# Four 2D scans at the end of a convolution stack: one-number reads ahead of the additions, half-tile row loads, a row-ordered result and moved early buffers

## Chip, cores and metric

One NeuronCore of one Trainium2 chip runs the whole program in one launch. The metric is device time in microseconds; the kernel before takes 9100.21 us (median of 3 runs, 9092.29 to 9107.42).

## What is computed

x has the shape [4, 48, 256, 256], float32. Layers 0 and 1 (an attention layer and a gated layer, both with convolutions) end as x2. Layers 2 and 3 are the scans; each normalizes its input by groups and adds the scan's result to it:

```python
def step(w, b):
    def f(carry, inp):
        nxt = inp + _conv1d(carry, w, b)      # 48 -> 48 channels, 5 taps along the line
        return (nxt, nxt)
    return f
# down over the rows, back up over them with the same weights,
# then right over the columns, then left: 4 x 256 dependent steps for each layer
x = x + _L2_conv_ref(_gn(x), ...)
x = x + _L3_conv_ref(_gn(x), ...)
```

Every step needs the line that the step before made, so a scan is a chain: multiplication on TensorE, addition on VectorE, the next multiplication.

## The kernel before

The four images form two pairs, and each pair is one generator, `chain(pair)` (L1015). A line is kept as 96 partitions (two neighbouring positions by 48 channels) by 2 images by 128 elements. `step` (L1037) makes one scan step: for each image i, three `nc.tensor.matmul` into a PSUM bank (L1045; the trace has two records for each, so 6 for a half step and 12 for a step), one `tensor_add` of PSUM and the input line into the next of four carry buffers (L1049 or L1053, NC = 4), then a callback `after` that files the line: ScalarE writes it with its bias into the row or column tile (L1127 down, L1168 up, L1248 right), and in the left scan GpSimd adds it to the residual (L1293, or L1297 into the `done` tile when it goes straight to the output: `direct`, L1271, layer 3 of the second pair). All of a step's engines wait for each other by semaphores that the framework places.

Tiles are slots of 16 KB a partition, five in a ring for each pair (`take`, L1012). In the down scan a tile of 32 rows is two slots (even and odd rows); `load_rows` (L1069) brings the next tile's two slots with 8 DMAs at row 0 of a tile, and `norm` (L1101, ScalarE, L1104) scales each quarter of them at rows 16, 20, 24 and 28. D, U and Rt are DRAM copies of the scans' results, stored tile by tile. Where the up scan ends and the right scan begins (the turn, L1150 to L1211), the first column block `column` is put together from U and from the tile at hand; later blocks are loaded from U (L1235). GpSimd copies each column to a contiguous `pre` tile three steps ahead (`fetch`, L1221, four buffers). In the left scan of layer 2, batch statistics of finished blocks run on VectorE between the steps (L1325).

The first pair's final result is stored in column blocks as `xs[2]` (L1309); `to_rows` (L1369) loads it again in pieces of 512 bytes, GpSimd (three) and ScalarE (one) copies it into row order (L1393, L1395), and it is stored (L1397). The second pair writes the output itself (`write`, L1312), 128 bytes at a time, and 64 bytes for the last two blocks.

The order: all DMAs of the scans are issued on SyncE's queue, in one static order. The framework lists instructions greedily: a list scheduler with a cost model places what is ready, by priority, which is program order unless `high_priority` moves it. Program order of the chains is at L1400 to L1415: the first loads of chain 0 with priority 1600 places earlier, the first loads of chain 1, 992 steps of chain 0 (`LEAD`), then both in turn, then the rest of chain 1 with a piece of `to_rows` at the steps in `times`. So chain 0 (layer 2) runs nearly alone from 3543 to 4990 us, both chains run together until about 7530 us, and chain 1 (layer 3) runs alone to the end.

Of the kernel before, what the change touches and what calls it, by code (L numbers as in the profile page):

```python
# [964 lines left out]
def scans(ctx, tc, xs, out, wts, biases, dram, k, coefs, lead, spare):  # L965
# [23 lines left out]
    work = pool("c_work", 2)  # L989
# [12 lines left out]
    HP = W // 2 + 2  # L1002

# [11 lines left out]
    def chain(pair):  # L1015
# [6 lines left out]
        at = [0]  # L1022

# [45 lines left out]
        def load_rows(layer, n, ts, k0, k1):  # L1069

            for r in range(2):
                v = rows_view(ts[r])
                for q in range(2):
                    for b in range(2):
                        nc.sync.dma_start(
                            v[q * C : (q + 1) * C, b, k0:k1].rearrange("c k h w -> c k (h w)"),
                            xs[layer][pair][
                                r * C : (r + 1) * C, b, 2 * k0 + q : 2 * k1 - 1 + q : 2, n * NH : (n + 1) * NH, :
                            ].rearrange("c k h w -> c k (h w)"),
                        )  # L1080

        def layer_of(layer, first):
# [18 lines left out]
            def norm(ts, r, b):  # L1101
                v = by_batch(ts[r])[:, b]
                g = biased[b]
                nc.scalar.activation(v, v, AF.Identity, bias=g[:, 1:2], scale=g[:, 0:1])  # L1104
# [7 lines left out]
            for r in range(2):  # L1112
                for b in range(2):
                    norm(now, r, b)
            for n in range(NT):
                ahead_ = None
                for r in range(RT):
                    if r == 0 and n + 1 < NT:
                        ahead_ = [slot("dn"), slot("dn")]
                        load_rows(layer, n + 1, ahead_, 0, NK)  # L1120
                    if ahead_ and r >= RT // 2 and r % 4 == 0:
                        i = (r - RT // 2) // 4
                        norm(ahead_, i // 2, i % 2)
# [7 lines left out]
                    else:  # L1131
                        step(layer, 0, inp, keep)
                    yield
# [8 lines left out]
            column = None  # L1142
            for n in reversed(range(NT)):
                ahead_ = None
                for r in reversed(range(RT)):
# [4 lines left out]
                    if n == 0 and r == RT // 4:  # L1150

                        column = slot("col")
                        v = cols_view(column)
                        for par in range(2):
                            for b in range(2):
                                h0 = NH + 1 - par
                                here = slice(par * C, (par + 1) * C)
                                nc.sync.dma_start(
# [381 lines left out]
```

## Time and profile before

| what | value |
|---|---|
| median of 3 runs | 9100.21 us (9092.29 to 9107.42) |
| profiled execution, its own time | 9095.42 us |
| its span, clock | 9093.6 us, 0.982 |
| busy share PE / DVE / ACT / POOL | 96% / 41% / 38% / 23% |
| records of the scans' matmuls (L1045) | 48960 |
| addition, 96x128 (L1049, L1053) | 286 to 288 ns |
| ScalarE's filing of a line (L1127, L1168, L1248) | 398 to 402 ns |
| GpSimd's addition (L1293), copy to `pre` (L1225), copy to rows (L1393) | 519, 644, 1130 ns |
| `norm` of a quarter tile (L1104) | 2081 ns, 128 of them |
| one-number copy or addition on VectorE (L1097, L1098) | 0.14 to 0.16 us |

In a line of a table by stretches stand: the stretch and its length, the busy time of PE with its records in brackets, the same for weight loads (PEld), the granted clock, the busy share of the DMA engines and GB/s. In a line of the timeline stand start, duration, engine (SPq: SyncE's queue; DVEq: VectorE's sequencer), line, operation and, in square brackets, the engine's idle time before it and what ended it. A merged line covers several instructions ("x2").

### The profile page before, as it was taken

The page shows a single profiled execution, that of the slowest core. Times are in us where ns is not written, and L with a number is a line of the kernel's source. Part 1 is how long each engine was busy: PE and PEld are TensorE (multiplying, and loading weights), DVE is VectorE, ACT ScalarE, POOL GpSimd, SP SyncE. Part 2 cuts the span into 40 slices and gives each one's busy share as a digit, 9 for nine tenths or more (in the row PEclk, how much of TensorE's full clock was granted, in tenths as well). Part 3 has the DMA queues.
Part 4 walks back from the last instruction along what each step waited for, and adds up shares of the span by engine and source line. Part 5 has one row for each costly group of instructions (what it writes and reads, how often), then busy time and mean ns, then how long its engine had stood idle before and what let it go on. Part 6 is the DMA issues. An engine that isn't in the chain of part 4 may idle for free.

```text
span 9093.6 us, 162344 instructions
## 1 busy us (share of the span) xinstructions
PE 8711.1 (96%) x62920; PEld 7268.3 (80%) x62920; DVE 3759.8 (41%) x10790; ACT 3489.6 (38%) x7033; POOL 2067.0 (23%) x3855
## 2 busy tenths in 40 slices
PE   6999999999999987999999999999999999999997
PEld 4777777433333345999999999999999999999997
DVE  3332010234555555444455444444445554343443
ACT  0011000123343355755511776665662004665510
POOL 0000000001111120002465000002446773002475
PEclk9999999999999988999999999999999999999998
DMA  7663323467878878655587773656556787888689
GB/s 150 132 135 87 74 59 73 97 136 168 181 171 187 177 165 165 149 133 128 145 211 178 157 147 95 160 129 160 154 152 177 218 227 169 172 183 201 175 173 168
DMA packets 1201990, 1390.61 MB, mean 153 GB/s; under 512 B 285712, under 2 KB 1128208, under 8 KB 1138240
## 3 DMA queue, kind: packets, MB, share of 16 engines
q1 hardware_dynamic: 1201120, 1379.90, 67.3%
q8 instruction: 493, 8.08, 0.4%
q14 instruction: 281, 2.30, 0.1%
q0 software_dynamic: 96, 0.33, 0.0%
HBM read 812.02 MB, written 509.61 MB: 145 GB/s over the span
## 4 chain that ended last, share of the span: by engine, by line
PE 88%; DMA 4%; DVE 3%; ACT 1%; issue 1%; SPq 1%; POOL 1%; DVEq 0%; POOLq 0%; ACTq 0%
PE ps L1045 57%; PE py L581 7%; PE acc L294 6%; PE acc L295 5%; PE acc L296 4%; PE py L590 3%; PE pt L276 1%; DMA stage<-x 1%; DMA tok<-x 1%; PE ph L698 1%; PE pout L868 1%; DMA x<-y 1%; PE ptok L751 1%; ACT x1n L541 1%; DMA sx<-in_x 1%
## 5 line engine op out<-in xcount | busy, mean ns | idle before, releaser
L1045 PE MATMUL ps<-carry,w 96*96 96x128 f32 x48960 | 5496.1, 275 | 75.6 <-DVE carry L1049 29.7
L1045 PEld LDWEIGHTS ps<-carry,w 96*96 96x96 f32 x48960 | 5445.9, 163 | 129.1 <-DVE carry L1053 39.6
L1225 POOL COPY pre<-col 96x256 f32<-96x256 f32 x1020 | 655.1, 644 | 2800.1 <-DMA col<-last 2011.7
L1248 ACT ACTIVATE lines<-carry,b 96x128 f32<-96x128 f32 (+1 forms) x2044 | 817.0, 402 | 618.8 <-DVE carry L1053 615.2
L1127 ACT ACTIVATE dn<-carry,b 96x128 f32<-96x128 f32 (+1 forms) x2044 | 770.1, 398 | 712.0 <-DVE carry L1049 709.2
L1049 DVE TENSOR_TENSOR carry<-ps,dn 96x128 f32<-96x128 f32 x2280 | 654.7, 288 | 900.5 <-PE ps L1045 806.8
L1053 DVE TENSOR_TENSOR carry<-ps,pre 96x128 f32<-96x128 f32 x2040 | 586.1, 287 | 798.7 <-PE ps L1045 544.8
L1168 ACT ACTIVATE up<-carry,b 96x128 f32<-96x128 f32 x1792 | 718.1, 402 | 480.1 <-DVE carry L1049 479.0
L1293 POOL TENSOR_TENSOR stage<-stage,carry 96x128 f32<-96x128 f32 (+1 forms) x1533 | 790.7, 519 | 314.2 <-DVE carry L1053 184.3
L1053 DVE TENSOR_TENSOR carry<-ps,lines 96x128 f32<-96x128 f32 x2040 | 576.2, 286 | 671.8 <-PE ps L1045 636.8
L1049 DVE TENSOR_TENSOR carry<-ps,up 96x128 f32<-96x128 f32 x1792 | 515.8, 288 | 678.9 <-PE ps L1045 667.9
L581 PE MATMUL py<-x1n,wy 128*96 128x512 f32 x1536 | 705.2, 609 | 29.1 <-ACT x1n L541 27.9
L295 PE MATMUL acc<-xs,xt 128*96 128x288 f32 x2048 | 666.4, 407 | 0.0
L294 PE MATMUL acc<-xt 128*96 128x288 f32 x2048 | 665.9, 408 | 0.0
L581 PEld LDWEIGHTS py<-x1n,wy 128*96 128x96 f32 x1536 | 245.2, 166 | 453.4 <-issue 436.1
L261 ACT ACTIVATE xn<-raw,coef 96x2048 f32<-96x2048 f32 x64 | 133.6, 2093 | 985.8 <-PE pt L276 818.2
L296 PE MATMUL acc<-xt,xs 128*96 128x192 f32 x2048 | 501.8, 327 | 0.0
L279 DVE COPY xt<-pt 128x384 f32<-128x384 f32 x256 | 136.5, 554 | 848.1 <-PE pt L276 649.4
L296 PEld LDWEIGHTS acc<-xt,xs 128*96 128x96 f32 x2048 | 332.0, 164 | 154.2 <-issue 1.2
L295 PEld LDWEIGHTS acc<-xs,xt 128*96 128x96 f32 x2048 | 331.8, 164 | 151.0 <-issue 2.0
L604 DVE TENSOR_TENSOR y<-py,t 96x512 f32<-96x512 f32 x256 | 171.4, 678 | 596.8 <-PE py L590 596.8
L590 PE MATMUL py<-x2n,wy 64*96 64x512 f32 x1536 | 363.0, 601 | 0.0
(179 smaller groups left out, 4823.8 us busy)
## 6 DMA issues: line engine op xcount, KB each, us to landing
stage<-x SPq DMA_DIRECT2D x64, 1536.0 KB
dn<-x SPq DMA_DIRECT2D x240, 384.0 KB
col<-U SPq DMA_DIRECT2D x60, 1536.0 KB
R<-lines SPq DMA_DIRECT2D x60, 1536.0 KB
lines<-R SPq DMA_DIRECT2D x60, 1536.0 KB
D<-dn SPq DMA_DIRECT2D x56, 1536.0 KB
up<-D SPq DMA_DIRECT2D x56, 1536.0 KB
U<-up SPq DMA_DIRECT2D x224, 384.0 KB
```

The source lines that it names most:

```text
L294: nc.tensor.matmul(acc[0], lhsT=xt[:, h + 2, :], rhs=xt[:, here, :], start=first, stop=last)
L295: nc.tensor.matmul(acc[1], lhsT=xt[:, h + 2, :], rhs=xs[:, here, :], start=first, stop=last)
L296: nc.tensor.matmul(acc[2], lhsT=xs[:, h + 2, :], rhs=xt[:, past, :], start=first, stop=last)
L581: nc.tensor.matmul(ps, lhsT=held["w"][0][:, dx], rhs=x1n[:, 2 * c : 2 * c + 2, dx : dx + W], start=dx == 0, stop=False)
L1045: nc.tensor.matmul(ps, lhsT=w_sb[layer][:, way, j, :], rhs=old[:, i, j : j + W // 2], start=j == 0, stop=j == 2)
L1049: nc.vector.tensor_add(new[:, i].rearrange("p (k w) -> p k w", w=KC), ps.rearrange("p (k w) -> p k w", w=KC), inp[:, i])
L1053: nc.vector.tensor_add(new[:, i], ps, inp[:, i])
L1127: nc.scalar.activation(inp[:, b], blocks(new[:, b]), AF.Identity, bias=bias[:, 0:1])
L1168: nc.scalar.activation(place[:, b], blocks(new[:, b]), AF.Identity, bias=bias[:, 1:2])
L1225: nc.gpsimd.tensor_copy(t, cols_view(block)[:, :, w % 2, :, w // 2])
L1248: nc.scalar.activation(line[:, b], new[:, b], AF.Identity, bias=bias[:, 2:3])
L1293: nc.gpsimd.tensor_add(to[:, b], to[:, b], new[:, b])
```

## The change

1. `look` reads one number of a place that ScalarE (down, up, right) filed three steps earlier into the tile `seen`, once after each step; in the right scan it reads a number of the next `pre` tile as well. In the left scan (not the direct one) VectorE reads a number of the residual at every second step, one such place later. The list is emptied at the start of each row tile and of each scan. In the left scan GpSimd adds both images in one operation.
2. `load_rows` loads one slot; at row 0 of tile n half tiles up to number 2n + 4 are asked for, half a tile more than before. `norm` comes at rows 11, 14, 22, 25.
3. At the turn the first two column blocks are put together from the tile at hand.
4. The first pair has three `pre` buffers instead of four, and fetches two steps ahead. The `work` pool has one buffer instead of two.
5. The first pair's layer 3 is stored as `result` in the order of row blocks, in pieces of 512 bytes, four DMAs a block; `to_rows` loads it in runs of 16 KB a partition. Its first 16 pieces have all four copies on GpSimd; the last 8 start at step 530 instead of 508.
6. The second pair writes the output 128 bytes at a time to the end.
7. Chain 0's first step has priority 1400 places earlier; chain 1's first loads come 64 steps ahead of the end of chain 0's lead.

```diff
...
     first_w = pool("c_first", 1)
     slots_a = pool("c_slot_a", 3)
     wp = pool("c_w", 1)
-    work = pool("c_work", 2)
+    work = pool("c_work", 1)
     slots_b = pool("c_slot_b", 1)
     slots_c = pool("c_slot_c", 1)
     slots_d = pool("c_slot_d", 5)
...
     NC = 4
     HP = W // 2 + 2
+    NY = H // 2 // (SLOT // W)
+    result = dram.tile([P, 2, NY, NK * 2, SLOT // (NK * 2)], F32, tag="result", name="result")
     w_sb, b_sb = [], []
     for layer in range(2):
         at = wp if layer else first_w
...
             nc.gpsimd.memset(c, 0.0)
         last = wp.tile([P, 2, W // 2], F32, tag=f"last{pair}", name=f"last{pair}")
         at = [0]
+        seen = wp.tile([P, 1], F32, tag=f"seen{pair}", name="seen")
+        kept = []
+        def look(place, fetched=None):
+            kept.append(place)
+            if len(kept) > 3:
+                if fetched is None:
+                    nc.vector.tensor_copy(seen, kept.pop(0))
+                else:
+                    nc.vector.tensor_add(seen, kept.pop(0), fetched)
         def slot(name):
             return take(pair, f"{name}{pair}")
...
         def row(ts, r):
             return rows_view(ts[r % 2])[:, :, :, r // 2, :]
...
+        def load_rows(layer, n, r, t, k0, k1):
...
         def layer_of(layer, first):
...
                 nc.vector.tensor_add(t[:, 1:2], g[:, 1:2], bias[:, 0:1])
                 biased.append(t)
...
             for n in range(NT):
                 ahead_ = None
                 for r in range(RT):
-                    if r == 0 and n + 1 < NT:
-                        ahead_ = [slot("dn"), slot("dn")]
-                        load_rows(layer, n + 1, ahead_, 0, NK)
-                    if ahead_ and r >= RT // 2 and r % 4 == 0:
-                        i = (r - RT // 2) // 4
-                        norm(ahead_, i // 2, i % 2)
+                    if r == 0:
+                        kept.clear()
+                        while len(halves) < min(2 * n + 5, 2 * NT):
+                            t = slot("dn")
+                            load_rows(layer, len(halves) // 2, len(halves) % 2, t, 0, NK)
+                            halves.append(t)
+                        if n + 1 < NT:
+                            ahead_ = halves[2 * n + 2 : 2 * n + 4]
+                    if ahead_ and r in (11, 14, 22, 25):
+                        norm(ahead_[r // 22], r % 11 // 3)
                     inp = row(now, r)
                     def keep(new, b):
...
                         keep(inner(), slice(0, 2))
                     else:
                         step(layer, 0, inp, keep)
+                    look(inp[:, 1, 0, 0:1])
                     yield
                 if ahead_:
                     for r in range(2):
...
             nc.scalar.activation(last, inner(), AF.Identity, bias=bias[:, 0:1])
-            column = None
+            columns = None
             for n in reversed(range(NT)):
                 ahead_ = None
+                kept.clear()
                 for r in reversed(range(RT)):
                     if r == RT - 1 and n > 0:
                         ahead_ = [slot("up"), slot("up")]
...
                             nc.sync.dma_start(ahead_[i], D[n - 1][i])
                     if n == 0 and r == RT // 4:
...
+                        columns = [slot("col") for _ in range(2)]
+                        for j in range(2):
...
+                    look(place[:, 1, 0, 0:1])
                     yield
                     if n == 0 and r < 2:
                         par, h0 = 1 - r, r
-                        v = cols_view(column)
+                        for j in range(2):
+                            v = cols_view(columns[j])
+                            for q in range(2):
+                                nc.sync.dma_start(
+                                    v[par * C : (par + 1) * C, :, q, h0 : h0 + NH, :].rearrange("c b h w -> c b (h w)"),
+                                    rows_view(now[r])[q * C : (q + 1) * C, :, j].rearrange("c b h w -> c b (h w)"),
+                                )
+                if n == 0:
...
+                    for j in range(2):
                         for q in range(2):
                             nc.sync.dma_start(
...
+                                cols_view(columns[j])[0:C, :, q, 0, :],
+                                last[q * C : (q + 1) * C, :, j * KC : (j + 1) * KC],
                             )
...
                 for r in range(2):
                     v = rows_view(now[r])
                     par = 1 - r
...
             for _ in range(3):
                 yield
-            x, y = xs[layer][pair], xs[layer + 1][pair]
+            x = xs[layer][pair]
+            y = xs[1][pair]
             stage = None
             fetched = {}
+            tags = [f"st{pair}0", f"st{pair}1"] + [f"pre{pair}{i}" for i in range(1 + pair)]
+            far = len(tags) - 1
             def fetch(block, n, w):
                 g = n * CB + w
-                tag = (f"st{pair}0", f"st{pair}1", f"pre{pair}0", f"pre{pair}1")[g % 4]
-                t = wp.tile([P, 2, W // 2], F32, tag=tag, name="pre")
+                t = wp.tile([P, 2, W // 2], F32, tag=tags[g % len(tags)], name="pre")
                 nc.gpsimd.tensor_copy(t, cols_view(block)[:, :, w % 2, :, w // 2])
                 fetched[g] = t
-            for w in range(1, 3):
+            kept.clear()
+            column = columns[0]
+            for w in range(1, far):
                 fetch(column, 0, w)
             for n in range(NK):
                 ahead_ = None
                 for w in range(CB):
-                    if w == 0 and n + 1 < NK:
+                    if w == 0 and n == 0:
+                        ahead_ = columns[1]
+                    elif w == 0 and n + 1 < NK:
...
                     if w == 0:
                         lines = slot("lines")
-                    if w + 3 < CB:
-                        fetch(column, n, w + 3)
+                    if w + far < CB:
+                        fetch(column, n, w + far)
                     elif ahead_ is not None:
-                        fetch(ahead_, n + 1, w + 3 - CB)
+                        fetch(ahead_, n + 1, w + far - CB)
                     line = lines_view(lines)[:, w]
                     def keep(new, b):
...
                         keep(inner(), slice(0, 2))
                     else:
                         step(layer, 1, fetched.pop(n * CB + w), keep)
+                    if n + 1 < NK or w + 1 < CB:
+                        look(line[:, 1, 0:1], fetched[n * CB + w + 1][:, 1, 0:1])
                     yield
                 if ahead_ is not None:
                     nc.sync.dma_start(Rt[n], lines)
...
+            kept.clear()
             direct = layer == 1 and pair == NP - 1
-            done, width = None, 0
+            done = None
             writes = []
             for n in reversed(range(NK)):
                 ahead_ = None
-                if direct and n < 2:
-                    done, width = take(0, "done").rearrange("p (b n) -> b p n", b=2), CB
-                elif direct and n % 2 == 1:
-                    done, width = [take(0, "done") for _ in range(2)], 2 * CB
+                if direct and n % 2 == 1:
+                    done = [take(0, "done") for _ in range(2)]
                 for w in reversed(range(CB)):
                     if w == CB - 1 and n > 0:
                         ahead_ = slot("lines"), slot("stage")
...
                         nc.sync.dma_start(by_batch(ahead_[1]), block_of(x, n - 1))
                     if layer == 0 and n == 0 and w == CB // 2:
                         following = [slot("dn"), slot("dn")]
-                        load_rows(1, 0, following, 1, NK)
+                        for r in range(2):
+                            load_rows(1, 0, r, following[r], 1, NK)
                     line = lines_view(lines)[:, w]
                     to = cols_view(stage)[:, :, w % 2, :, w // 2]
                     def keep(new, b):
                         if not direct:
-                            nc.gpsimd.tensor_add(to[:, b], to[:, b], new[:, b])
+                            if b.stop == 2:
+                                nc.gpsimd.tensor_add(to, to, new)
                             return
                         for i in range(b.start, b.stop):
-                            place = done[i].rearrange("p (h w) -> p h w", w=width)[:, :, n * CB % width + w]
+                            place = done[i].rearrange("p (h w) -> p h w", w=2 * CB)[:, :, n % 2 * CB + w]
                             nc.gpsimd.tensor_add(place, to[:, i], new[:, i])
                     if n == NK - 1 and w == CB - 1:
                         keep(inner(), slice(0, 2))
                     else:
                         step(layer, 2, line, keep)
+                    if not direct and w % 2:
+                        kept.append(to[:, 1, H // 2 - 1 :])
+                        if len(kept) > 1:
+                            nc.vector.tensor_copy(seen, kept.pop(0))
                     if late:
                         late.pop(0)()
-                    if writes and (w % 4 == 0 if n < 2 else w % 8 == 4):
+                    if writes and w % 8 == 4:
                         writes.pop(0)()
                     yield
-                if not direct:
+                if layer == 0:
                     nc.sync.dma_start(block_of(y, n), by_batch(stage))
-                elif n * CB % width == 0:
-                    def write(b, r, done=done, width=width, w0=n * CB):
+                elif not direct:
+                    v = stage.rearrange("p (b q t n) -> p b q t n", b=2, q=2, t=NY)
+                    for b in range(2):
+                        for q in range(2):
+                            nc.sync.dma_start(result[:, b, :, 2 * n + q], v[:, b, q])
+                elif n % 2 == 0:
+                    def write(b, r, done=done, w0=n * CB):
...
                     writes += [lambda b=b, r=r, f=write: f(b, r) for b in range(2) for r in range(2)]
...
                 yield following
...
-    def to_rows(pair):
-        y = xs[2][pair]
+    def to_rows(pair, engines):
         nh = SLOT // W
         to = out[rows(pair)].rearrange("p (h w) -> p h w", w=W)
-        for n in range(H // 2 // nh):
+        for n in range(NY):
             got = []
             for r in range(2):
                 t = take(pair, "oi")
                 for b in range(2):
                     nc.sync.dma_start(
-                        t[b * C : (b + 1) * C].rearrange("c (k n) -> c k n", k=2 * NK),
-                        y[r * C : (r + 1) * C, b, :, n * nh : (n + 1) * nh, :].rearrange("c k h w -> c k (h w)"),
+                        t[b * C : (b + 1) * C], result[r * C : (r + 1) * C, b, n].rearrange("c k n -> c (k n)")
                     )
                 got.append(t.rearrange("p (k q h w) -> p k q h w", k=NK, q=2, w=KC))
             yield
...
                 for i in range(4):
                     r, q = i // 2, i % 2
                     dst, src = v[:, :, r, :, :, q], got[r][:, :, q, here, :].rearrange("p k h w -> p h k w")
-                    if i < 3:
-                        nc.gpsimd.tensor_copy(dst, src)
+                    if engines[i] is nc.scalar:
+                        nc.scalar.copy(dst, src)
                     else:
-                        nc.scalar.copy(dst, src)
+                        engines[i].tensor_copy(dst, src)
...
     with tc.high_priority(offset=1600):
         next(chains[0])
-    next(chains[1])
-    for _ in range(lead):
+    with tc.high_priority(offset=1400):
+        next(chains[0])
+    for i in range(1, lead):
+        if i == lead - 2 * RT:
+            next(chains[1])
         next(chains[0])
     while next(chains[0], True) is None:
         next(chains[1])
-    pieces = to_rows(0)
-    times = [20 + 26 * i for i in range(16)] + [508 + 28 * i for i in range(8)]
+    engines = [nc.gpsimd] * 4
+    pieces = to_rows(0, engines)
+    times = [20 + 26 * i for i in range(16)] + [530 + 24 * i for i in range(8)]
     for i, _ in enumerate(chains[1]):
+        if i == times[16]:
+            engines[3] = nc.scalar
         if i in times:
             next(pieces, None)
     assert next(pieces, True) is True
...
-        for i in (2, 3, 4)
+        for i in (2, 3)
     ]
     def gated(ctx, tc, banks, p_small):
```

## Prediction

> **What bounds the kernel now.** I read the busy shares and the chain of work that ended last first.
>
> ```profile
> PE 8711.1 (96%) x62920; PEld 7268.3 (80%) x62920; DVE 3759.8 (41%) x10790; ACT 3489.6 (38%) x7033; POOL 2067.0 (23%) x3855
> ...
> PE 88%; DMA 4%; DVE 3%; ACT 1%; issue 1%; SPq 1%; POOL 1%; DVEq 0%; POOLq 0%; ACTq 0%
> ```
>
> TensorE looks full, and 57% of the chain is L1045, the scans. But a pipelined matmul counts as busy while it waits, so I take the rate of records instead: the table by stretches, for L1045 alone.
>
> ```profile
> 3510.00:3543.00 33.00, 4.79 (x18) 3.74 (x18) 0.50 1.13 184
> 3600.00:4200.00 600.00, 600.00 (x5356) 597.96 (x5354) 1.00 0.62 137
> 4240.00:4580.00 340.00, 340.00 (x2971) 331.32 (x2970) 1.00 0.54 148
> 4990.00:6200.00 1210.00, 1210.00 (x11054) 1209.86 (x11053) 1.00 0.62 136
> 7720.00:7950.00 230.00, 210.66 (x1801) 207.90 (x1800) 0.94 0.82 172
> 7950.00:8300.00 350.00, 348.94 (x3099) 345.75 (x3098) 1.00 0.88 193
> 8300.00:8370.00 70.00, 54.33 (x431) 52.99 (x429) 0.88 0.79 166
> 8370.00:8680.00 310.00, 310.00 (x2708) 302.00 (x2707) 1.00 0.67 180
> 9010.00:9093.60 83.60, 36.55 (x296) 35.99 (x294) 0.70 0.98 122
> ```
>
> With both chains, 4990 to 6200, a record takes 1210 / 11054 = 109.46 ns: TensorE's own pace. **Excess** of a stretch is its length less its records times 109.46 ns. Chain 0 alone: down and up 3600 to 4200, 600 - 586.3 = 13.7 us (112.0 ns a record); right 4240 to 4580, 14.8 us (114.4 ns). Chain 1 alone: rest of down 32.9, up 10.8, turn 22.8, right 13.6. The start has 31.0, the end 51.2. From the same view: left of chain 0 (4580 to 4915) 18.3, the change of layer (4915 to 4990) 15.9, chain 1's down from 7630 to 7720 2.3, 4200 to 4240 1.0, direct left 4.0 and 17.8. The two-chain stages, 2.4 ms, have nothing to win. All that this change can win is some 250 us.
>
> Why are single chains slower than 109.46? Lines L1049 (up, 4000 to 4200) and L1053 (right, 4300 to 4500):
>
> ```profile
> L1049 DVEq EVENT_SEMAPHORE  x297: 21/21/589, 4000.2 to 4199.3; - x149
> L1049 DVE TENSOR_TENSOR carry<-ps,up x295: 286/288/291, 4000.3 to 4198.0; 96x128 f32<-96x128 f32 x148
> ```
>
> ```profile
> L1053 DVEq EVENT_SEMAPHORE  x291: 21/21/50, 4300.1 to 4499.5; - x146
> ...
>   ACT lines L1248: 66.7, 145
>   PE ps L1045: 49.8, 146
> ```
>
> Each addition has a wait instruction of its own ahead of it. In the records the instruction waits for TensorE and the addition for ScalarE (its old reader of the carry buffer). Over 3,672 such additions down and up, the addition starts 379 ns after the half step's last matmul record started; over some 270 that wait for TensorE directly (mostly after a statistic in chain 0's left scan), 309 ns. In the right scan every second one, with three waits, starts at 408 ns: its idle time is 66.7 / 145 = 0.46 us instead of 0.34.
>
> **What the Trainium skill says.** "VectorE: DVE Perf Modes", on the errata of trn2, says that small SBUF operations pay a fixed cost whatever their size; the trace agrees: one number costs 0.14 to 0.16 us (L1097, L1098), 128 columns 0.29. "TensorE: Matmul & The Clock Gate", Part 1, says that an idle window of some 3.4 us halves the clock until about as much work has been done; the trace agrees: after the 10 us gap at 8342 the next half steps take 1.27 us, then 0.66. "DMA: Bandwidth & Descriptors", Anatomy of one DMA, says that a semaphore wait happens on the issuing sequencer before dispatch: one blocked transfer holds the queue. The trace agrees below. No page that I found prices an additional wait instruction; the trace does.
>
> **1. Reads ahead of the additions.** A half step's loop is its six records, 0.657 us, plus what lies from the last record to the next multiplication. Up takes 12 x 112.0 = 1.344 us a step, so that rest is 0.687; TensorE is busy with the other half for 0.657 of it. Taking 70 ns away leaves 0.617: the stall of 31 ns a step goes, and TensorE is late next. Right: 12 x 114.4 - 657 = 0.716, less 99 ns is 0.617 too. The same wait for ScalarE's step t-3 is now in the read, which VectorE reaches while TensorE works. It adds about 3,200 instructions of 0.15 us, 480 us on VectorE, in the 0.37 us that it is idle ahead of an addition; without that cover each would cost its 0.15. Behind a read stands, with two chains, the other chain's addition. Four steps of 32 in a row tile keep their own wait, since the list is emptied, so down and up give 7/8: chain 0 (13.7 + 1.0) x 7/8 = 12.9, right 14.5 of 14.8; chain 1 up 9.5, right 13.3; down's steady part, 2.6 ns x 2,602 records x 7/8 = 5.8 (2,602 are those of 7630 to 7950). Together **56**. Left of chain 0 has additions behind statistics of 0.68 us, which stay; one GpSimd operation in place of two (519 ns each) is bounded by 519 and 1038 ns and is hidden by four carry buffers. Bounds -5 to +8, I take **3**. The direct left scan gets no reads: 0.
>
> **2. Half tiles.** SyncE's queue in chain 1's down scan:
>
> ```profile
> 7818.31 0.31 SPq L1136 DMA_DIRECT2D D<-dn  x1
> 7845.85 0.33 SPq L1397 DMA_DIRECT2D out<-oo  x1
> 7846.23 0.42 SPq L1136 DMA_DIRECT2D D<-dn  x1
> 7846.74 22.87 SPq L1075 DMA_DIRECT2D dn<-x  x8
> ```
>
> The output store at 7845.85 waited 27 us for ScalarE's copy (L1395), and the next rows' loads stood behind it; the chain then shows 10.7 us of loading and two `norm`s of 2.1 us at the tile's edge, and TensorE restarts slowly. Every edge here has such a pair of `norm`s. The first 16 output pieces now stay off ScalarE, half a tile more is loaded ahead, and `norm` is 5 and 3 rows earlier. Of 32.9 less the steady 4.6 I take two thirds, **19** (0 to 26). The total of loads is the same; each takes 2.1 to 2.9 us of issue. ScalarE's `norm`s at rows 11 and 14 leave a backlog of 2.1 + 2.1 - 3 x 0.51 = 2.6 us (0.8 of 1.31 us a step is its filing), under the 3 steps = 3.9 us that the reads allow.
>
> **3. The turn.**
>
> ```profile
> 8336.42 1.22 SPq L1235 DMA_DIRECT2D col<-U  x2
> 8350.77 1.80 POOL L1225 COPY pre<-col 96x256 f32<-96x256 f32 x3 [14.43 <-DMA col<-U]
> 8351.43 0.48 DVE L1053 TENSOR_TENSOR carry<-ps,pre 96x128 f32<-96x128 f32 x2 [10.36 <-POOL pre L1225]
> ```
>
> The second block could be loaded only once U was stored; now it is on chip. That removes 10.4 us and five slow half steps, 5 x 0.61 = 3.1: **13**. The first block's wait (4 us) stays; its small DMAs are joined by six others of about 0.6 us, hidden by the last step (0 to 2 us).
>
> **4. Row order.** The 64 stores in 512-byte pieces (768 each) cost 2.1 us of queue each, as U<-up does (12.64 us for 6), about 134 us less 16 x 0.6 in chain 0's left scan, beside two chains with a step every 2.6 us. The loads of `to_rows`, 15 us of queue for 4, nearly vanish where chain 1 is alone. Value 0 here, -30 if the queue there is fuller than the DMA share of 0.79 suggests; its benefit is in part 2.
>
> **5. End.** After the last load the queue issues twelve output stores in 71.3 us: four of 768 KB (32), then eight of 384 KB in 64-byte pieces (40). Now eight of 768 KB; the last four, at 5.6 to 8 us, take 22 to 32 in place of 40, but can start only after the last step. **10** (-5 to 15). Before that the queue needs 24.3 us for a block of 16 steps (two output stores 18.2, loads 6), over their 21: unchanged.
>
> **6. Start.** From 3510 to 3543 TensorE waits in order for chain 1's first line (idle 9.06 us, then 7.2), while chain 0 has used up its first tile. With the second tile and half the third asked for earlier, chain 0 can run there: **20** of 31 (0 to 40, as it could also fill gaps before 3510). Fewer `pre` buffers for pair 0: 0, GpSimd's 0.64 us has 1.3 us. Change of layer: 3.
>
> **Sum:** 56 + 3 + 19 + 13 + 10 + 20 + 3 = 124. The profiled execution's 9095.4 gives 8971; it lies 4.8 us below the median shown, so **8976**.
>
> **Rivals.** *A: scheduling keeps start and edges* (20 + 19 + 3 not won): 9018. The list is static and greedy, and nothing in the profile shows that the slots for half a tile more are free early. *B: the additions keep a second wait* (some other reader needs ScalarE): 8976 + 59 = 9035. Against it: additions that wait for TensorE alone exist in this trace. *C: chain 1, started later, no longer fills chain 0's gaps*: it made 37 half steps at the turn and some 68 from 4600 to 5000, 105 x 0.657 = 69 us: 9045. *D, slower: the reads stop VectorE in order behind `norm`.* If ScalarE's backlog passes three steps, the read holds the additions of both chains; each of 128 `norm`s then costs its 2.08 us, 266 in all: 8976 + 266 = 9242. It decides from 124 / 2.08 = 60 stopped `norm`s on. My backlog of 2.6 us against 3.9 speaks against it, additions that waited for L1127 in down (44 times, 16.4 us, 5000 to 5500) for it.
>
> **Chances.** Forecast 0.54, A 0.18, B 0.08, C 0.07, D 0.07; B with C near 9090, no visible change, 0.06. What a measurement here can tell from no change is about 0.2%, 18 us. Faster 0.87, same 0.06, slower 0.07. The forecast's own range is 8925 to 9010; with A, B and C the range is 8925 to 9055.
>
> **What would show it.** 109.5 ns a record in 3600 to 4580 and in chain 1's up and right; additions without a wait instruction; no 14 us wait of `pre` for U at the last turn; no pairs of `norm` at tile edges; a tail under 35 us after the last matmul. Wrong would be: right still at 114 ns (B), additions that wait long for L1104 (D), fewer chain 1 rows before 4990 (C).

## The result, and the profile after

| kernel | median (range), runs | ratio to before, 95% interval |
|---|---|---|
| before | 9099.5 us (9092.29 to 9107.42), 12 | |
| changed | 9098.14 us (9084.97 to 9105.45), 12 | 0.9996 (0.9987 to 1.0005) |

No change that can be measured, where 8976 was forecast. The profiled execution of the changed kernel took 9105.24 us, its span is 9103.5 us (before: 9095.42 and 9093.6).

The busy shares of the changed kernel: VectorE has 3,241 instructions more, the reads. Their durations add up to 486 us, as the prediction had it (480), but VectorE is busy only 212 us longer, since a read can start before the addition ahead of it ends (in the timeline below at 3991.72, where the addition that started at 3991.52 takes 0.29 us).

```profile
PE 8713.5 (96%) x62920; PEld 7234.4 (79%) x62920; DVE 3971.3 (44%) x14031; ACT 3440.2 (38%) x7023; POOL 1948.2 (21%) x3100
```

Its chain of work that ended last covers some 6% of the span, so it tells little; I read the rate of records again. The table by stretches for the scans' matmuls (L1064 now), at the times at which the changed kernel is in each stage: chain 0's up, right and left, both chains, chain 1's up and right.

```profile
3600.00:4150.00 550.00, 549.60 (x5017) 548.85 (x5016) 1.00 0.67 149
4240.00:4560.00 320.00, 301.27 (x2476) 276.11 (x2476) 1.00 0.46 127
4640.00:4960.00 320.00, 291.92 (x2459) 271.63 (x2458) 1.00 0.65 180
5060.00:6200.00 1140.00, 1138.82 (x10408) 1138.47 (x10407) 1.00 0.58 138
8020.00:8340.00 320.00, 320.00 (x2921) 319.49 (x2920) 1.00 0.73 177
8420.00:8700.00 280.00, 275.50 (x2495) 273.02 (x2494) 1.00 0.71 198
```

The left scan of chain 0 in the kernel before, for comparison:

```profile
4580.00:4915.00 335.00, 329.26 (x2893) 321.29 (x2892) 1.00 0.82 213
```

Length over records: down and up of chain 0 fell from 112.0 to 550 / 5017 = 109.6 ns a record, chain 1's up from 112.9 to 109.6. But chain 0's right scan **rose** from 114.4 to 129.2 ns, and its left scan from 335 / 2893 = 115.8 to 130.1 ns. Chain 1's right scan fell from 114.5 only to 112.2.

Where reads work, chain 0's up scan (changed kernel) looks as forecast. Most wait instructions are gone: 23 are left beside 269 additions from 4000 to 4180, where the kernel before had one for each:

```profile
L1068 DVE TENSOR_TENSOR carry<-ps,up x269: 286/288/290, 4000.0 to 4176.0; 96x128 f32<-96x128 f32 x135
L1068 DVEq EVENT_SEMAPHORE  x23: 21/21/653, 4007.9 to 4179.3; - x23
```

The timeline, which doesn't list wait instructions, shows that the read lies inside the time that VectorE would be idle:

```profile
3991.52 0.29 DVE L1068 TENSOR_TENSOR carry<-ps,up 96x128 f32<-96x128 f32 x1 [0.37 <-PE ps L1064]
3991.72 0.14 DVE L1039 COPY seen<-up 96x1 f32<-96x1 f32 x1
3992.17 0.29 DVE L1068 TENSOR_TENSOR carry<-ps,up 96x128 f32<-96x128 f32 x1 [0.31 <-PE ps L1064]
```

Where it loses, chain 0's right scan (changed kernel), the timeline shows something else:

```profile
4340.32 0.48 DVE L1072 TENSOR_TENSOR carry<-ps,pre 96x128 f32<-96x128 f32 x2
...
4340.65 2.92 PE L1064 MATMUL ps<-carry,w 96*96 96x128 f32 x24 [0.18 <-DVE carry L1072]
4340.93 0.64 POOL L1259 COPY pre<-col 96x256 f32<-96x256 f32 x1 [0.72 <-DVE carry L1072]
4341.60 0.16 DVE L1041 TENSOR_TENSOR seen<-lines,pre 96x1 f32<-96x1 f32 x1 [0.81 <-POOL pre L1259]
4341.68 0.28 DVE L1072 TENSOR_TENSOR carry<-ps,pre 96x128 f32<-96x128 f32 x1
```

The additions at 4340.32 free a `pre` buffer; GpSimd starts its copy into that buffer at 4340.93; and the very next instruction on VectorE is the read, which waits 0.81 us for this copy. The addition of the next half step stands behind it in VectorE's order, and TensorE stops (0.18 us ahead of the 24 records shown). The read was written two steps later in the program. In the order in which VectorE ran its instructions, 245 of the 252 reads of chain 0's right scan (layer 2) stand exactly two steps ahead of the place where they are written. (A timeline line at which x2 additions stand merges both additions of a step.) The page adds it up over the right scans of both chains: 437 us of VectorE's idle time ended with GpSimd's copy.

```profile
L1041 DVE TENSOR_TENSOR seen<-lines,pre 96x1 f32<-96x1 f32 x1008 | 166.8, 165 | 479.6 <-POOL pre L1259 437.2
```

The left scan of chain 0 has the same picture with GpSimd's addition. There 97 of the 127 reads (layer 2) stand two steps early, the other 30 one and a half.

```profile
4719.56 0.86 POOL L1334 TENSOR_TENSOR stage<-stage,carry 96x256 f32<-96x256 f32 x1 [0.42 <-DVE carry L1072]
...
4720.46 0.15 DVE L1348 COPY seen<-stage 96x1 f32<-96x1 f32 x1 [0.97 <-POOL stage L1334]
4720.53 0.47 DVE L1072 TENSOR_TENSOR carry<-ps,lines 96x128 f32<-96x128 f32 x2
4720.86 2.65 PEld L1064 LDWEIGHTS ps<-carry,w 96*96 96x96 f32 x24 [0.60 <-DVE carry L1072]
```

**Theory.** The framework's list scheduler places a read as soon as its operands' writers are placed, not where it is written. So in these two scans it stands right behind the additions that GpSimd's copy or GpSimd's addition is waiting for, and in VectorE's order it holds up the next additions until that work is done. **Rivals**: the reads' own 0.14 to 0.17 us on VectorE; the third `pre` buffer that is gone, reads or not; chain 0 lacking work from the other chain.

### The profile page after: what moved, and what is told of

The parts are those of the page before. It is cut to its first block, busy times and chain, and to the rows that moved or that the text cites. A ratio compares the mean times of both kernels' runs of the same rounds, so it can differ in the third digit from the quotient of the medians.

```text
span 9103.5 us, 158554 instructions
## 1 busy us (share of the span) xinstructions
PE 8713.5 (96%) x62920; PEld 7234.4 (79%) x62920; DVE 3971.3 (44%) x14031; ACT 3440.2 (38%) x7023; POOL 1948.2 (21%) x3100
## 5 line engine op out<-in xcount | busy, mean ns | idle before, releaser
L1064 PE MATMUL ps<-carry,w 96*96 96x128 f32 x48960 | 5490.2, 274 | 115.0 <-DVE carry L1072 71.7
L1064 PEld LDWEIGHTS ps<-carry,w 96*96 96x96 f32 x48960 | 5407.4, 163 | 207.4 <-DVE carry L1072 134.7
L1286 ACT ACTIVATE lines<-carry,b 96x128 f32<-96x128 f32 (+1 forms) x2044 | 780.2, 399 | 690.8 <-DVE carry L1072 650.1
L1334 POOL TENSOR_TENSOR stage<-stage,carry 96x256 f32<-96x256 f32 x768 | 656.2, 856 | 527.4 <-DVE carry L1072 497.5
L1072 DVE TENSOR_TENSOR carry<-ps,lines 96x128 f32<-96x128 f32 x2040 | 547.6, 283 | 424.9 <-PE ps L1064 401.1
L1072 DVE TENSOR_TENSOR carry<-ps,pre 96x128 f32<-96x128 f32 x2040 | 550.9, 284 | 271.1 <-PE ps L1064 239.7
L1041 DVE TENSOR_TENSOR seen<-lines,pre 96x1 f32<-96x1 f32 x1008 | 166.8, 165 | 479.6 <-POOL pre L1259 437.2
```

The costliest lines, as they stand in the source:

```text
L1064: nc.tensor.matmul(ps, lhsT=w_sb[layer][:, way, j, :], rhs=old[:, i, j : j + W // 2], start=j == 0, stop=j == 2)
L1072: nc.vector.tensor_add(new[:, i], ps, inp[:, i])
L1286: nc.scalar.activation(line[:, b], new[:, b], AF.Identity, bias=bias[:, 2:3])
L1334: nc.gpsimd.tensor_add(to, to, new)
```

## The experiments

All leave what is computed as it is. "Before" was 9095.16 us beside the first four, 9102.04 beside the next four, 9100.42 beside the last three.

**1. All reads held at their place.** `tc.issue_after` queues an instruction behind another on the same engine, in order only.

```diff
-                    nc.vector.tensor_add(new[:, i], ps, inp[:, i])
+                    made[0] = nc.vector.tensor_add(new[:, i], ps, inp[:, i])
...
-                    nc.vector.tensor_add(seen, kept.pop(0), fetched)
+                    with tc.issue_after(made[0].ins):
+                        nc.vector.tensor_add(seen, kept.pop(0), fetched)
```

(the same for the two other kinds of read)

> Every read is queued on VectorE behind the second addition of the step in whose place it is written, so the scheduler cannot put it earlier; nothing else differs from the changed kernel. Theory (reads placed two steps early stop VectorE for GpSimd's copy in pair 0's right scan and for GpSimd's addition in the left scan; 46 and 38 us lost there): both stages of chain 0 go from 129-130 to 110-113 ns a record, the reads no longer wait for GpSimd, and the time falls to 8990-9020 us. Rival 1 (the reads' own 0.14-0.17 us on VectorE is what costs): no change, 9090-9105. Rival 2 (chain 0 alone is short of work from the other chain, whatever the reads do): no change in these stages. Rival 3 (the three buffers alone cost): the right scan stays at 125-130 ns, the left one recovers, 9050-9065.

Measured: 8976.26 us (8973.9 to 8982.31), ratio 0.9869 (0.9855 to 0.9884). The stretches of this kernel, chain 0's right and left and chain 1's right scan:

```profile
4240.00:4500.00 260.00, 259.66 (x2363) 258.37 (x2362) 1.00 0.53 145
4600.00:4860.00 260.00, 254.28 (x2241) 245.98 (x2239) 1.00 0.71 195
8300.00:8560.00 260.00, 259.57 (x2363) 258.53 (x2362) 1.00 0.72 200
```

Right is at 110.0 ns in both chains, left at 116.0. In its timeline of chain 0's right scan the read follows 0.21 us behind the start of the addition and waits for nothing:

```profile
4300.19 0.28 DVE L1075 TENSOR_TENSOR carry<-ps,pre 96x128 f32<-96x128 f32 x1 [0.37 <-PE ps L1067]
4300.40 0.14 DVE L1044 TENSOR_TENSOR seen<-lines,pre 96x1 f32<-96x1 f32 x1
...
4300.61 0.65 POOL L1262 COPY pre<-col 96x256 f32<-96x256 f32 x1 [0.67 <-DVE seen L1044]
4300.85 0.29 DVE L1075 TENSOR_TENSOR carry<-ps,pre 96x128 f32<-96x128 f32 x1 [0.30 <-PE ps L1067]
```

VectorE's 14,031 work instructions are as many as in the changed kernel and the three buffers are the same, but the time is 122 us less; 251 of the 252 reads of this scan now stand where they are written. All three rivals fall as the cause of the loss by themselves: the reads' own time is still there, the third buffer is still gone, and the chains are the same.

**2. Four buffers for pair 0, reads free.**

```diff
-            tags = [f"st{pair}0", f"st{pair}1"] + [f"pre{pair}{i}" for i in range(1 + pair)]
+            tags = [f"st{pair}0", f"st{pair}1"] + [f"pre{pair}{i}" for i in range(2)]
```

> Pair 0 copies its columns ahead through four buffers again (three steps ahead), with the reads where the changed kernel has them. Theory: a read placed two steps early then names a copy that could start a whole step before, so pair 0's right scan falls from 129 to 110-115 ns a record (38 to 50 us), its left scan stays at 130, and the time is 9045-9065 us. Rival 1 (the reads' own time on VectorE): no change, 9090-9105. Rival 3 (buffers alone): the same 9045-9065, told from the theory by the first run, where the buffers stay three.

Measured: 9043.72 us (9031.92 to 9055.22), ratio 0.9946 (0.9929 to 0.9962). Its right and its left scan of chain 0:

```profile
4240.00:4560.00 320.00, 315.26 (x2852) 312.13 (x2851) 1.00 0.55 149
4640.00:4960.00 320.00, 293.85 (x2494) 275.17 (x2493) 1.00 0.65 174
```

Right 112.2 ns, left still 128.3. The scheduler now puts most reads 2.5 steps early (243 of 252), yet the copy they name can start one step sooner, and the wait shrinks to 0.15 us, inside VectorE's idle time. So in the right scan the loss needs both: the early read, and three buffers in place of four.

**3. No reads in right and left.** 

```diff
-                    if n + 1 < NK or w + 1 < CB:
-                        look(line[:, 1, 0:1], fetched[n * CB + w + 1][:, 1, 0:1])
...
-                    if not direct and w % 2:
-                        kept.append(to[:, 1, H // 2 - 1 :])
-                        if len(kept) > 1:
-                            nc.vector.tensor_copy(seen, kept.pop(0))
```

> The reads of the right scan and of the left scan are taken out, those of the down and up scans stay; three buffers for pair 0. Theory: chain 0's right scan comes back to the 114.4 ns and the left one to the 116 ns of the kernel before, so 84 us less lost there; chain 1's right scan goes from 111 back to 114 (8 us more): 9015-9035 us. Rival 3 (three buffers alone cost): the right scan stays at 125-130 ns even without its reads, 9055-9075. Rival 2 (chain 0 alone, whatever the reads do): 9095-9105.

Measured: 9013.1 us (9004.94 to 9017.37), ratio 0.9908 (0.9893 to 0.9922). Slightly better than expected; three buffers without reads cost nothing that can be seen (340 us hold 2961 records from 4240 to 4580, 114.8 ns; before 114.4).

**4. No reads at all**: the rest of the change by itself. As 3, and also

```diff
-                    look(inp[:, 1, 0, 0:1])
...
-                    look(place[:, 1, 0, 0:1])
```

> All reads are taken out; half tiles, row order at the turn, one GpSimd addition per step, early buffers and the end stay as changed. This prices the rest of the change alone. Theory: chain 0's and chain 1's stages go at the tempo of the kernel before (112 ns down and up, 114.4 right, 116 left, 113 chain 1's up), and the rest is worth what the stretches of the trace show after the left scan, some 35-45 us of which none is at the start: 9050-9070 us. The prediction had 65 us for the same parts (9035). Rival (the rest brings nothing): 9095-9105.

Measured: 9038.62 us (9035.69 to 9047.3), ratio 0.9938 (0.9924 to 0.9953). The rest is worth 56 us, more than expected: I had come down to 35 to 45 from the changed kernel's trace, and the prediction's own 65 was nearer.

**5. As 1, with the left scan's reads free.** Against run 1:

```diff
-                            with tc.issue_after(made[0].ins):
-                                nc.vector.tensor_copy(seen, kept.pop(0))
+                            nc.vector.tensor_copy(seen, kept.pop(0))
```

> As the first run (every read queued behind its own step's addition), but the left scan's reads are left to the scheduler again, which puts them two steps early, right behind the additions whose result GpSimd is then adding. Theory: only chain 0's left scan goes back to 130 ns a record, 38 us lost there and some 4 in the two-chain stages, so 9012-9022 us. Rival (the first run's gain came from the pin in some other way, such as a shifted order of VectorE's whole list): the left scan stays at 116 ns, 8970-8985.

Measured: 9033.09 us (9026.75 to 9039.27), ratio 0.9925 (0.991 to 0.994), 57 us above run 1 instead of 36 to 46. Some 6 us of that can be drift, since the kernel before was 7 us slower beside this run; by the ratios the distance is (0.9925 - 0.9869) x 9100 = 51 us. Its left scan takes 130.1 ns (260 us hold 1999 records from 4640 to 4900), its right scan 109.9 (240 us, 2183 records): the mechanism is as stated and the rival falls. The left scan itself loses 38 us against run 1. Of the rest of the 57 us between the two traces, some 6 lie at the end of the right scan, where the left scan already begins, 6 in the two-chain stages and 8 at the start, which differs from execution to execution.

**6. An older place for the left read.** This tells "too near in the text" from "placed as early as possible".

```diff
-                        if len(kept) > 1:
+                        if len(kept) > 3:
```

> The changed kernel, except that the left scan's read takes a place that is two entries older (four steps of the scan), so that as written it comes some 5 us after GpSimd's addition. Theory (the scheduler puts a read as early as its operand lets it, so that it stands behind the same addition whatever its age, and the wait is for GpSimd's addition of that very step): nothing is won, chain 0's left scan stays at 128-131 ns a record, 9090-9105 us. Rival (the place of the read in the text counts, and three more steps of distance are enough): the left scan falls to 116 ns, 9055-9065.

Measured: 9102.02 us (9093.39 to 9120.57), ratio 1.0003 (0.9994 to 1.0011). In VectorE's order 93 of chain 0's 125 left reads (layer 2) stand six steps early instead of two, behind the same addition as ever, and the rest four or more. The rate is 320 / 2415 = 132.5 ns from 4640 to 4960. Distance in the program is no cure here; an order that is enforced is (run 1).

**7. As 1, old order at the start.**

```diff
-    with tc.high_priority(offset=1400):
-        next(chains[0])
-    for i in range(1, lead):
-        if i == lead - 2 * RT:
-            next(chains[1])
+    next(chains[1])
+    for _ in range(lead):
         next(chains[0])
```

> As the first run, with the order at the start undone: chain 0's second step has no raised priority and chain 1's first loads are asked for ahead of chain 0's lead, as in the kernel before. The prediction had 20 us for the earlier start of chain 0: 8996. The trace of the first run shows chain 0 some 10 us ahead at its 904th record, the changed kernel's 5 us behind at the same place, so I expect 5 to 15 us: 8980-8990. Rival (the start is set by the stage before it, and the order brings nothing): 8972-8980.

Measured: 8971.74 us (8963.42 to 8977.67), ratio 0.9857 (0.9842 to 0.9872), not told apart from run 1, as the two intervals overlap. My 5 to 15 us was read from single executions and is a miss: the new order brings nothing that can be measured.

**8. As 1, no left reads, list kept over row tiles.** Against run 1, beside the left reads of run 3 taken out:

```diff
             for n in range(NT):
...
                     if r == 0:
-                        kept.clear()
...
             for n in reversed(range(NT)):
                 ahead_ = None
-                kept.clear()
```

with one `kept.clear()` ahead of each of the two scans.

> As the first run, without the left scan's reads, and with the list of places kept from one row tile to the next, so that every addition of down and up has its read. Theory: the left reads are worth nothing, since the statistics between the additions take the wait there, and the last eighth of the waits in down and up is worth (13.0 + 10.1 + 5.8) / 7 = 4 us: 8968-8976. Rival (the reads at a tile's edge hold the next tile's loads back by three rows): a loss of up to 10 us at the edges, 8976-8990.

Measured: 8973.89 us (8971.14 to 8978.75), ratio 0.9861 (0.9845 to 0.9878): the same as run 1. That the left reads are worth nothing fits; the 4 us for the last eighth of the waits is too small to be seen.

**9. The kernel before plus held reads in down, up and right, nothing else.** `look` as in run 1, with its list cleared at each row tile and scan, and its three calls:

```diff
                         step(layer, 0, inp, keep)
+                    look(inp[:, 1, 0, 0:1])
...
                         step(layer, 0, place, keep)
+                    look(place[:, 1, 0, 0:1])
...
                         step(layer, 1, fetched.pop(n * CB + w), keep)
+                    if n + 1 < NK or w + 1 < CB:
+                        look(line[:, 1, 0:1], fetched[n * CB + w + 1][:, 1, 0:1])
```

> The kernel before with nothing of the change but the reads of the down, up and right scans, each queued behind its own step's second addition; no reads in the left scan, four buffers for both pairs. The prediction's first part, alone: 12.9 + 14.5 + 9.5 + 13.3 + 5.8 = 56 us, 9095-9102 less 56. The runs so far, 62 us between the kernel without reads and the one with pinned reads: 9035-9045. Rival (the reads need the rest of the change, or the rest is what wins): above 9070.

Measured: 9031.9 us (9022.33 to 9034.36), ratio 0.9924 (0.991 to 0.9939): 68.5 us. The reads need nothing else of the change.

**10. The same with free reads.** Against run 9, in both branches of `look`:

```diff
-                    with tc.issue_after(made[0].ins):
-                        nc.vector.tensor_add(seen, kept.pop(0), fetched)
+                    nc.vector.tensor_add(seen, kept.pop(0), fetched)
```

> The same kernel, its reads left to the scheduler, which puts them 2.5 to 3 steps early. Theory: with four buffers GpSimd's copy could begin a step earlier, and ScalarE's filing is done by then or nearly so, so that an early place costs at most the 4 to 5 us seen in the run with four buffers: 9036-9050. Rival (any early place costs some 40 us in the right scan): 9075-9095.

Measured: 9031.33 us (9028.09 to 9043.99), ratio 0.9928 (0.9914 to 0.9943). With four buffers an early place costs nothing that the time shows; in chain 1's right scan its trace has 111.7 ns (200 us, 1791 records) against 109.8 with held reads.

**11. All that did not hurt, together, with four buffers.** The edits of runs 1, 2, 7 and 8 together.

> All that did not hurt, put together: pinned reads, none in the left scan, the list kept over row tiles, the old order at the start, four buffers for pair 0. Theory: the right scan of chain 0 gains 2 us at most from the fourth buffer, everything else is as it was: 8964-8976 us. Rival (the fourth buffer moves others and costs the start again, as the run with four buffers hints): 8976-8985.

Measured: 8983.62 us (8973.21 to 8986.47), ratio 0.9871 (0.9854 to 0.9887). A miss, in the rival's range, though its interval overlaps those of runs 1, 7 and 8. Its trace is some 11 us behind run 1's at 7630, 6 of them from the start and 5 from chain 0's left scan. Why is open: the fourth buffer may move others, and that was not taken apart. Runs 1, 7 and 8, all with three buffers, have the lowest medians, 1.3 to 1.4% below the kernel before; the simplest of them is run 1.

## Why the prediction was wrong, point by point

Each trace holds the same 48,960 records of the scans' matmuls. I take the time at which each kernel starts the n-th record, for the n that the kernel before has reached at a stretch's end, and give what is won on the kernel before within the stretch (us; single executions; where chains are mixed a few us move from row to row).

| stretch (times of the kernel before) | predicted | changed | no reads (4) | held reads (1) | before + held reads (9) |
|---|---|---|---|---|---|
| start, to 3600 | 20 | -4.9 | 1.7 | 9.7 | -5.3 |
| chain 0 down and up, to 4240 | 12.9 | 7.4 | -1.3 | 14.2 | 13.9 |
| chain 0 right, to 4580 | 14.5 | **-45.4** | -3.0 | 11.6 | 15.1 |
| chain 0 left, to 4915 | 3 | **-38.4** | -3.1 | -0.3 | 0.0 |
| change of layer, to 4990 | 3 | 8.7 | 7.7 | 11.8 | 1.3 |
| both chains, to 7630 | 0 | -8.5 | 0.6 | 1.7 | 3.4 |
| chain 1 down, to 7950 | 19 + 5.8 | 20.2 | 10.5 | 17.9 | 9.1 |
| chain 1 up, to 8300 | 9.5 | 10.5 | 0.1 | 10.1 | 10.5 |
| turn, to 8370 | 13 | 12.6 | 12.7 | 13.4 | 2.4 |
| chain 1 right, to 8680 | 13.3 | 6.8 | 0.0 | 12.3 | 12.7 |
| direct left, to the last matmul | with the end | 8.6 | 9.3 | 5.2 | 5.2 |
| from the last matmul to the end | 10 | 12.6 | 12.9 | 13.9 | -2.7 |
| sum | 124 | -9.8 | 48.1 | 121.5 | 65.7 |

**The step that failed** is in part 1, with its twin in part 6: "the same wait for ScalarE's step t-3 is now in the read, which VectorE reaches while TensorE works", and "Fewer `pre` buffers for pair 0: 0, GpSimd's 0.64 us has 1.3 us". Both take the read to stand in VectorE's order where it is written. The left scan's reads were priced at nothing in the same way: part 1 names no wait of theirs for GpSimd's addition. The section on the kernel says that the list is greedy; the step did not apply that to the reads themselves. They were placed two steps early, where GpSimd's 0.64 us copy had not 1.3 us but none: it starts only when the addition directly ahead of the read has freed the buffer. Right: 12 x (129.2 - 110.0) ns = 0.23 us a step, times the 255 steps of one scan 58.8 us, against the 45.4 + 11.6 = 57.0 us between the two runs in the table. Left: 12 x (130.1 - 116.0) = 0.17 us a step, 43 us, against 38.1 us (38.4 less 0.3) and those 6 at the border to the right scan. In the two-chain stages, too, the changed kernel lost 8.5 us where held reads won 1.7. The Trainium skill, "PSUM — Partial Sum Buffer", Engine vs sequencer instructions, says that the queues of ScalarE, VectorE and GpSimd are strict FIFO; the trace agrees: at 4341.68 an addition starts as soon as the read has waited its 0.81 us out, though it doesn't use what the read waited for.

**The wait's price was right.** With held reads (run 1) 7,224 additions have no wait instruction ahead and start 309 to 310 ns after the start of the last record of their half step (medians of four groups); the 857 with one such instruction start 379 ns after it (median), as 7,724 of the kernel before do; run 1 less run 4 is 62 us, run 9 68.5, for the 56 predicted. Chain 0's 12.9 was 14.2, its right scan's 14.5 11.6 to 15.1, chain 1's 9.5 and 13.3 were 10.1 and 12.3. The 3 us for the left scan were none: without its reads it lost 2.7 to 3.1 (runs 3 and 4), with held ones 0.3.

**Half tiles** 19: the rest of the change, without reads, gives 10.5 in chain 1's down scan. With held reads it is 17.9, of which the reads alone give 9.1 (run 9), so 9 to 11: about half of what I took, within its 0 to 26. **Turn** 13: 12.7. One stall is left of two, the first block's wait. I had it at 4 us and up to 2 more; TensorE's idle time there was 4.03 us (ahead of 8317.32) and is now 6.48 us, while VectorE waits for the first block's last DMA (`col<-last`). The changed kernel:

```profile
8368.96 0.85 DVE L1290 TENSOR_SCALAR carry<-col,b 96x256 f32<-96x256 f32 x1 [5.16 <-DMA col<-last]
8369.95 32.40 PE L1064 MATMUL ps<-carry,w 96*96 96x128 f32 x264 [6.48 <-DVE carry L1290]
```

**Row order** cost nothing, as taken: the two-chain stages differ by 0.6 us without reads. **End** 10: the tail after the start of the last matmul went from 45.6 to 33.0 us, 12.6. The 5 to 9 us ahead of it belong at least in part to no step of mine, since run 9, which changes nothing there, has 5.2 too. **Change of layer** 3: 8 to 12 in the changed kernel and runs 1 and 4, but -2.0 in run 7; why is open.

**Start** 20: not won (run 7). The gap in the kernel before lies right behind the end of the stage before the scans; I counted it as free time to fill. With the new order chain 0's steps did run earlier, but between that stage's matmuls, in TensorE's order. Its last group of matmuls (L868), first in the kernel before, then in run 1:

```profile
3506.93 3.31 PE L868 MATMUL pout<-g,w_sb 32*96 32x512 f32 x6 [3.56 <-DVE y L879]
```

```profile
3534.51 2.29 PE L868 MATMUL pout<-g,w_sb 32*96 32x512 f32 x6
```

The stage ends at 3536.8 instead of 3510.2, and what waits for it (the coefficients of chain 1's norm) comes 27 us later. The other traces go the same way: where 570 or more scan records come ahead of the stage's end (seven traces with the new order) it lies at 3536.7 to 3552.1, where 396 to 486 do (the kernel before, runs 2, 7, 9, 10 and 11) at 3509.9 to 3525.1. Run 2 has the new order in the program and yet belongs to the second group: its fourth buffer was enough to change the list. That this is why nothing was won is read from the traces; no run changed it by itself.

**The rivals.** B (the additions keep a second wait) and C did not happen. A was half right: the start was not won, the tile edges were, by half. D had the right form and the wrong place: reads do stop VectorE in order, behind GpSimd's copies and additions of chain 0's right and left scans, not behind ScalarE's `norm`. Near no change ended not by one small effect, as the text's last 0.06 had it, but by 84 us lost in two stages against 74 us net won elsewhere; that the two nearly cancel is chance. So in part is run 1's 8976.26 us, the very number forecast: its start won 9.7 in place of 20, and nothing by run 7, half tiles about half of their 19 and the left scan nothing, while the change of layer (11.8 for 3), the direct left scan (5.2 for 0), the end (13.9 for 10) and the reads themselves (62 for 56) gave more.

## What to carry to other kernels

An instruction that is there only to take a wait early is worth what the wait cost only if it stands where its operand is surely ready; under a list scheduler it can drift, as it did here, to the first place where the operand's writer has been listed, and holds all that is queued behind it. Tie it behind an instruction of the right age by an order-only edge, and look at its place in the compiled order before counting its cover. When lookahead buffers are cut in the same change, count the slack from where the reader stands, not from where the value is used.

## What was not expected of the hardware

- An addition with a wait instruction of its own ahead of it starts 70 ns later than one without (379 against 309 ns from the last matmul record), in run 1 as in the kernel before; a one-number read that takes the wait over cost nothing that can be seen where it lay in VectorE's 0.37 us of idle time (run 1, right scan, 4240 to 4500: 160 ns mean, 1.0 us of idle time ahead of all 196 reads).
- 0.81 us of idle time ahead of each read slowed the right scan's step by only 0.23 us (run 1 has two idle stretches of 0.37 and 0.30 us in such a step, which the wait takes the place of). In the left scan 0.97 us at every second step cost 0.17 us a step.
- GpSimd's addition of 96 x 256 takes 856 ns, against twice 519 ns for two of 96 x 128.
